# A two-layer relational graph convolution: six treatments of TensorE at its signals in layer 2

## Chip, cores and metric

The kernel runs on one core of a Trainium2 chip. Times are device microseconds (us) of one execution; below, PE is TensorE's matmuls, PEld its weight loads, DVE is VectorE, ACT is ScalarE, POOL is GpSimd and SP is SyncE.

## The reference

12500 nodes with 128 features, 200000 edges sorted by their destination, 8 relations. Two layers of a relational graph convolution, each with a residual, then one more residual and a layer norm:

```python
def _rgcn_conv(x, src, dst, et, basis, comp, root, bias):
    W = jnp.einsum('rb,bio->rio', comp, basis)
    xw = jnp.einsum('ni,rio->nro', x, W)
    msgs = xw[src, et]
    seg = dst * N_REL + et
    summed = jax.ops.segment_sum(msgs, seg, num_segments=N_NODES * N_REL)
    cnt = jax.ops.segment_sum(jnp.ones((msgs.shape[0],), x.dtype), seg, num_segments=N_NODES * N_REL)
    mean = summed / jnp.maximum(cnt, 1.0)[:, None]
    agg = mean.reshape(N_NODES, N_REL, HIDDEN).sum(axis=1)
    return agg + x @ root + bias
...
for l in range(N_LAYERS):
    h_new = _rgcn_conv(h, src, dst, edge_type, basis[l], comp[l], root[l], bias[l])
    h_new = jax.nn.relu(h_new)
    h = h_new + h
...
x = _layernorm(x + h, axis=-1)
```

(The last line is the reference's, with the convolutions' result called h.)

## The kernel before

The edges lie in 1563 tiles of 128, and eight tiles make an octet: 196 octets in each layer. The kernel works through the octets in order, layer 1 and then layer 2. For each octet POOL issues eight indirect DMAs (`gather`, L677), each of which fetches 128 rows of 128 floats into a ring of seven buffers `rows`; a buffer is asked for again five octets ahead of its use. In layer 1 the rows come from `x`, and the means of each destination and relation are multiplied by the relation's weights. Layer 1 also makes the table `y_d`, in which every node's row is already multiplied by each of the eight weights, so layer 2 gathers rows of `y_d` and only has to average and add them.

In layer 2 an octet q below 192 (`FULL`) goes through these steps:

- DVE makes the one-hot matrices `sT` and `pl` two octets ahead (`slot_hots`, L1090 and L1093).
- `slot_sums(q)` (L1428) is eight fp32 matmuls (L1441; each is recorded as two passes) of `rows` with `sT` into one part of the bank `po`. The last of them signals. It waits for the gathers of the octet, for DVE, and for ACT's copy of the octet before, since all octets use the same part of the bank.
- ACT copies the sums to `ys` (L627, by `copy`), and signals.
- `place_sums(q)` (L1449) adds `ys` to the accumulator `s` of the current block of nodes with a matmul by `pl` (L1466), and at a block's end also the root term (L1470). It stands on PE one octet late: PE's order is `slot_sums(q)`, `place_sums(q-1)`, then `slot_sums(q+1)`.
- At the end of a block DVE takes the accumulator (L1298, L1302, L1322), and every eight blocks four transposes at a time on PE (L1573) and the layer norm on DVE follow.

A buffer of `rows` comes free for the next gather when `slot_sums` of its octet has signalled, so POOL waits on PE's signals, ACT waits on them for the copy, and DVE for its matrices and for the accumulators. POOL's next gathers stand behind a waiting one on its queue.

The order on each engine is that in which the Python code calls `plan.add`. `Plan` works out, for each operation, which counts of which engines it must wait for, and `Plan.emit` (L395 to L408) writes the waits, the operation, and, where a count is waited for, `then_inc` on the engine's semaphore: a signal that the operation itself sends as it completes. `plan.mark("PE")` makes the last operation added a signalling one. An operation of PE never waits for PE.

Of the kernel before, what the change touches and what calls it, by code (L numbers as in the profile page):

```python
# [300 lines left out]
class Plan:  # L301
# [25 lines left out]
    def add(self, eng, emit, reads=(), writes=(), lane=None, n=1, after=()):  # L327


        raw, war = {}, {}  # L330
        writes = list(writes) + [c for c in reads if c[0] in self.banks]

        def need(d, op):
            proc, at = self.ops[op][0:2]
            d[proc] = max(d.get(proc, 0), at)

        me = len(self.ops)
        for c in (*reads, *after):
            if c in self.writer:
                need(raw, self.writer[c])  # L340
        for c in writes:
            if c in self.writer:
                need(raw, self.writer[c])
            for op in self.readers.get(c, ()):
                need(war, op)
        for c in reads:
            self.readers.setdefault(c, []).append(me)
        for c in writes:
            self.writer[c] = me
            self.readers[c] = []  # L350
        if lane is not None:
            k, i = self.lanes[lane]
            proc = (lane, i)
            self.lanes[lane][1] = (i + 1) % k
            if self.count[proc]:
                need(war, self.last[proc])
            step = 16 * n
        else:
            proc, step = eng, 1
            if eng == "PE":  # L360
                raw.pop(eng, None)
                war.pop(eng, None)
        known = self.known[eng]
        waits = {}
        for d, exact in ((raw, True), (war, False)):
            for p, at in d.items():
                if known.get(p, 0) >= at or waits.get(p, 0) >= at:
                    continue
                if p in self.signals and (self.lazy or not exact):
                    later = [a for a in self.signals[p] if a >= at]  # L370
                    at = min(later) if later else at
                waits[p] = max(at, waits.get(p, 0))
        for p in list(waits):
            for o in waits:
                if o != p and self.seen[o, waits[o]].get(p, 0) >= waits[p]:
                    del waits[p]
                    break
        for p, at in waits.items():
            if p in self.signals:
                self.signals[p].add(at)  # L380
            for o, a in self.seen[p, at].items():
                known[o] = max(known.get(o, 0), a)
            known[p] = max(known.get(p, 0), at)
        self.count[proc] += step
        at = self.count[proc]
        self.seen[proc, at] = dict(known)
        if lane is not None:
            self.last[proc] = me
        self.ops.append((proc, at, eng, emit, waits))

    seen = None
    last = None
    banks = ("ps", "py", "po", "pt", "ct")

    def emit(self):  # L395
        value = {e: {a: i + 1 for i, a in enumerate(sorted(s))} for e, s in self.signals.items()}
        end = max(i for i, op in enumerate(self.ops) if op[2] == "SP")
        for i, (proc, at, eng, emit, waits) in enumerate(self.ops):
            if i == end:
                self.landed(False)  # L400
            for p, a in sorted(waits.items(), key=str):
                self.engines[eng].wait_ge(self.sems[p], value[p][a] if p in value else a)
            ins = emit()
            if proc != eng:
                for x in ins if isinstance(ins, list) else [ins]:
                    x.then_inc(self.sems[proc], 16)
            elif at in value[eng]:
                ins.then_inc(self.sems[eng], 1)  # L408
    def landed(self, stores):

        for p in self.last:
# [18 lines left out]
def ordered_path(  # L430
# [25 lines left out]
    nc = tc.nc  # L456
# [31 lines left out]
    SOLO = 50  # L488
    FLAG = 100
    SOON = 16  # L490
    DONE = NT - 4
    FULL = NQ - 4
    assert D == P and R * K == P and B == BF + 1 and 1 < TL and LAST < P and BF % 4 == 0 and Q == G and N % 2 == 0
# [111 lines left out]
    nb_f = keep([1, 1], F32, "nb_f")  # L605

    plan = Plan(tc, {"hw": 8, "aq": 4, "gq": 4})
    plan.seen, plan.last = {}, {}

    def vec(emit, reads=(), writes=()):  # L610
        plan.add("DVE", emit, reads, writes)
# [4 lines left out]
    def pe(emit, reads=(), writes=()):  # L616
        plan.add("PE", emit, reads, writes)
# [815 lines left out]
    def slot_sums(q):  # L1433
        t, c = rows_g.pop((1, q))
        d, dc = dms2.pop(q)
        b, bc = misc
        m0 = b[:, 3, :]

        def emit():
            for i in range(Q):  # L1440
                last = nc.tensor.matmul(m0[i // 2 * 2 * K:(i // 2 + 1) * 2 * K, :], d[:, i, :], t[:, i, :],  # L1441
                                        start=i % 2 == 0, stop=i % 2 == 1)
            return last

        pe(emit, [c + (0,), c + (1,), dc], [bc, ("done", 1)])
        plan.mark("PE")
        o, oc = ys[q] = ys_r.take()
        copy(o, m0, [bc], [oc])
        plan.mark("ACT")  # L1449

    def place_sums(q, k, opens, last):
        t, c = pl.pop(q)
        o, oc = ys.pop(q)
        a, ac = acc[k]
        root_in = opens and k >= 0
        reads = [c, oc]
        m = P
        if root_in:
            ht, hc = hb[k]
            reads += [hc, ("w", 1, R)]  # L1460
        fixed = q == SOON // Q
        if fixed:
            reads += fix_rows_c + fix_dm_c

        def emit():
            ins = nc.tensor.matmul(a, o[:m], t[:m], start=opens, stop=last and not root_in and not fixed)  # L1466
            if fixed:
                ins = nc.tensor.matmul(a, fix_rows, fix_dm, start=False, stop=last and not root_in)
            if root_in:
                ins = nc.tensor.matmul(a[:, :rows_of(k)], w_sb[:, 1, R, :], ht[:, :rows_of(k)], start=False, stop=last)  # L1470
            return ins

        pe(emit, reads, [ac])
        plan.mark("PE")

    def add_rows(q, k, opens, last, between_last=None):
        t, c = rows_g.pop((1, q))
# [363 lines left out]
    for q in range(NQ):  # L1841
        near_end = q >= FULL
        if q == FLAG:
            load_flag()
        plan.lazy = not near_end
        k = sup(q)
        if gathers(1, q):
            pool(lambda: nc.gpsimd.drain())
        opens, last = opened_by(q)
        if opens:  # L1850
            acc[k] = acc_b[k % 2]
        if q == NQ - 1:
            last_st = st_r.take()
            turn, stats, one_by, scale = zip(*(last_norm(i) for i in range(2)))
            add_rows(q, k, opens, last, turn[0])
            stats[0]()
            for step in finish(1, k):
                step()
            turn[1]()
            one_by[0]()  # L1860
            stats[1]()
            scale[0]()
            one_by[1]()
            scale[1]()
            break
        if q == NQ - 2:
            first_sums()
        if q == 0:
            check_all()
        late = q - 1  # L1870
        if q < FULL:
            slot_sums(q)
        if 0 <= late < FULL:
            place_sums(late, sup(late), *opened_by(late))
        if q >= FULL:
            add_rows(q, k, opens, last)
        onehot(1, q + 2)
        if sup(q + 2) != sup(q + 1) and q + 2 < NQ:
            open_block(sup(q + 2))
        if todo:  # L1880
            todo.pop(0)()
        for i in range(2):
            for j, step in ending:
                step()
                plan.mark("DVE")
                n = j // S
                if j >= 0 and j % S == S - 1:
                    norm(n)
                    if n + 2 < NX:
                        todo.extend([lambda: None] * 2 + [lambda n=n: load_x(n + 2)])  # L1890
            ending.clear()
            if q == NQ - 2:
                if i == 0:
                    add, close_it, carry_on = finish(1, k, True)
                    for step in (carry_on, add, close_it):
                        step()
            elif i == 0:
                for j in [late] * (0 <= late < FULL) + [q] * (q >= FULL):
                    if opened_by(j)[1]:
                        a, b = finish(1, sup(j))  # L1900
                        a()
                        ending.append((sup(j), b))
            if not near_end:
                break
        while near_end and todo:
            todo.pop(0)()

# [64 lines left out]
```

## Time and profile before

| what | value |
|---|---|
| runs | 4581.87, 4591.37, 4590.76 us; median 4590.76 |
| the profiled execution | 4590.46 us, span 4588.4 us |
| granted TensorE clock, mean of the span | 0.665 |
| busy over the span | POOL 64%, PE 42%, PEld 33%, DVE 30%, ACT 10% |
| gathers of layer 2 | first at 2320.7, last at 4571.9 us |

The profile is of one execution. Its page gives each engine's busy time, the span in 40 slices (each digit a busy share in tenths; PEclk is the clock that the throttle granted to TensorE), and groups of instructions by line. A group's row has the busy time, the mean of one in ns, and the idle time of the engine just ahead of its instructions with what ended most of it; "remote" is a release that the profile puts down to none of the core's recorded instructions at that moment, and "issue" a wait for nothing that it shows. In the timeline a row is the start, the time taken, the engine, the line, the operation, and in brackets the idle time ahead of it. The end of a matmul is modelled.

### The profile page before, as it was taken

What the parts mean: (1) busy time and instruction counts of PE and PEld (TensorE: products, weight loads), DVE (VectorE), ACT (ScalarE), POOL (GpSimd) and SP (SyncE); (2) the same over time, 40 slices, a digit from 0 to 9 for tenths busy, and PEclk for the clock granted to TensorE, in tenths of its full rate; (3) what the DMA queues carried; (4) which work ended last, traced back from release to release, by engine and by line L of the source; (5) the groups of instructions that cost most, each with busy time, mean ns of one, the idle gap of its engine ahead of it and who ended that gap; (6) DMA issues with size and microseconds to landing.
All of it is one profiled execution on the core that took longest, in us unless ns stands there. A gap on an engine that the chain in (4) does not pass through costs nothing.

```text
span 4588.4 us, 33820 instructions
## 1 busy us (share of the span) xinstructions
PE 1941.5 (42%) x11751; PEld 1512.2 (33%) x11751; DVE 1384.9 (30%) x4891; ACT 466.3 (10%) x1141; POOL 2953.3 (64%) x3135
## 2 busy tenths in 40 slices
PE   2666756666566666656731122222222222222213
PEld 1555555555455555545521111111111111111112
DVE  2544333333333323233321222222222222222224
ACT  0111112121111111111210000000000000000000
POOL 5666666666666666666556666666666666666665
PEclk9878778787777777777865555555555555555556
DMA  3111122232222222222221111212212212122121
GB/s 100 45 50 46 46 62 87 87 92 92 88 69 73 74 69 74 64 66 70 78 71 45 47 51 52 56 46 57 55 47 55 56 47 56 46 56 55 47 55 50
DMA packets 129812, 284.69 MB, mean 62 GB/s; under 512 B 54019, under 2 KB 61773, under 8 KB 129637
## 3 DMA queue, kind: packets, MB, share of 16 engines
q0 software_dynamic: 100064, 205.13, 17.2%
q10 hardware_dynamic: 16971, 52.05, 3.0%
q1 hardware_dynamic: 12602, 25.31, 1.6%
q8 instruction: 94, 1.54, 0.1%
q14 instruction: 81, 0.66, 0.0%
HBM read 223.63 MB, written 58.65 MB: 62 GB/s over the span
## 4 chain that ended last, share of the span: by engine, by line
another core or an unknown queue 64%; PE 20%; issue 8%; ACT 5%; DVE 2%; DMA 0%; POOL 0%; SPq 0%; ACTq 0%; POOLq 0%; DVEq 0%
PE y L1246 7%; PE s L1214 5%; ACT sT L627 2%; PE pt L1345 2%; PE po L1441 2%; ACT ys L627 1%; PE po L1277 1%; DVE dm L1121 1%; ACT y_row L627 1%; PE ct L1345 1%; PE ct L870 0%; PE po L1279 0%; PE ct L871 0%; PE pt L1183 0%
## 5 line engine op out<-in xcount | busy, mean ns | idle before, releaser
L677 POOL DMA_INDIRECT rows<-in_x_dram,idx x1563 | 1476.1, 944 | 841.7 <-issue 440.2
L677 POOL DMA_INDIRECT rows<-y_d,idy x1563 | 1475.1, 944 | 742.6 <-issue 453.3
L1441 PE MATMUL po<-rows,sT 128*32 128x128 f32 x3072 | 206.3, 411 | 1571.3 <-ACT ys L627 1151.2
L1246 PE MATMUL y<-w_sb,sT 128*128 128x128 f32 x3136 | 542.3, 345 | 526.2 <-ACT ys L627 198.6
L1246 PEld LDWEIGHTS y<-w_sb,sT 128*128 128x128 f32 x3136 | 509.4, 254 | 551.6 <-ACT ys L627 207.6
L1121 DVE TENSOR_SCALAR dm<-cols,kr,w 128x128 f32<-128x128 f16 x1563 | 526.2, 403 | 494.2 <-remote 203.1
L1441 PEld LDWEIGHTS po<-rows,sT 128*32 128x32 f32 x3072 | 121.9, 155 | 1658.1 <-ACT ys L627 1190.5
L1090 DVE TENSOR_SCALAR sT<-cols,kr,w 128x32 f32<-128x32 f16 x1536 | 352.8, 303 | 762.9 <-remote 617.7
L1214 PEld LDWEIGHTS s<-dm,rows 128*128 128x128 f32 x3126 | 436.3, 217 | 161.0 <-ACT sT L627 86.5
L1214 PE MATMUL s<-dm,rows 128*128 128x128 f32 x3126 | 450.5, 302 | 64.9 <-ACT sT L627 40.8
L627 ACT ACTIVATE sT<-s 128x512 f32<-128x512 f32 x391 | 212.5, 596 | 783.0 <-remote 556.8
L627 ACT ACTIVATE ys<-po 128x128 f32<-128x128 f32 x192 | 53.2, 277 | 2087.1 <-remote 1936.5
L1298 DVE TENSOR_TENSOR s<-s,carry 128x128 f32<-128x128 f32 x97 | 28.9, 298 | 670.8 <-remote 455.7
L1298 DVE TENSOR_TENSOR po<-po,carry 128x128 f32<-128x128 f32 x98 | 29.2, 298 | 655.1 <-remote 454.7
L1345 PE MATMUL pt<-w_sb,arena 128*128 128x512 f32 x258 | 157.3, 682 | 62.4 <-issue 50.0
L1466 PE MATMUL s<-pl,ys 128*128 128x256 f32 x288 | 167.9, 684 | 0.0
L1277 PE MATMUL po<-pl,ys 128*128 128x256 f32 x392 | 139.4, 440 | 24.2 <-issue 15.8
L627 ACT ACTIVATE y_row<-pt 128x512 f32<-128x512 f32 x131 | 78.4, 598 | 682.0 <-remote 484.2
L870 PE MATMUL ct<-arena,id_h 128*128 128x512 f16 (+1 forms) x188 | 75.5, 421 | 84.4 <-DVE arena L860 37.1
L860 DVE TENSOR_TENSOR arena<-cols,arena 128x129 f16<-128x129 f16 (+62 forms) x188 | 73.6, 408 | 69.5 <-remote 65.5
L1129 DVE TENSOR_SCALAR pl<-cols,pos 128x256 f32<-128x256 f16 x196 | 93.1, 476 | 0.0
L1466 PEld LDWEIGHTS s<-pl,ys 128*128 128x128 f32 x288 | 69.7, 301 | 53.3 <-issue 53.3
(212 smaller groups left out, 1409.7 us busy)
## 6 DMA issues: line engine op xcount, KB each, us to landing
y_d<-y_row ACTq DMA_DIRECT2D x96, 512.0 KB
rows<-in_x_dram,idx POOLq DMA_INDIRECT x1563
rows<-y_d,idy POOLq DMA_INDIRECT x1563
x_g<-in_x_dram SPq DMA_DIRECT2D x24, 512.0 KB
out_dram<-x_g SPq DMA_DIRECT2D x12, 512.0 KB
arena<-in_L_gnn_basis_dram SPq DMA_DIRECT2D x2, 512.0 KB
w_d<-y_row SPq DMA_DIRECT2D x2, 512.0 KB
w_sb<-w_d SPq DMA_DIRECT2D x2, 512.0 KB
```

Source lines behind the costliest of these rows:

```text
L627: act(lambda: nc.scalar.activation(out_t, in_t, AF.Copy), reads, writes)
L677: ins.append(nc.gpsimd.indirect_dma_start(out=t[:, i - q * Q, :], out_offset=None, in_=table_t, in_offset=bass.IndirectOffsetOnAxis(ap=ids ...
L870: nc.tensor.matmul(ct[:, :nb, :], id_h, eq[:, s - s0, :nb, main], start=(s == 1), stop=False)
L1090: vec(in_turn([lambda i=i: nc.vector.tensor_scalar(t[:, i, :], cols[:, :2 * K], kr[:, i0 + i:i0 + i + 1], w[:, i0 + i:i0 + i + 1], op0=ALU ...
L1121: emits.append(lambda i=i: nc.vector.tensor_scalar(t[:, i - q * Q, :wide], cols[:, :wide], ids[:, i:i + 1], w[:, i:i + 1], op0=ALU.is_equa ...
L1129: emits.append(lambda: nc.vector.tensor_scalar(o[:m], cols[:m], pos[:m, g // (2 * R), g % (2 * R):g % (2 * R) + 1], None, op0=ALU.is_equal))
L1214: last = nc.tensor.matmul(s_b[i // 4][0][:, i % 4, :], t[:, i, :], d[:, i, :], start=True, stop=True)
L1246: last = nc.tensor.matmul(y[:m], t[:, r, :nt, :].rearrange("p t k -> p (t k)"), w_sb[:, 0, r, :], start=(r == 0), stop=(r == R - 1))
L1277: ins = nc.tensor.matmul(a, o[:m], t[:m], start=opens, stop=last and not root_in)
L1345: pe(lambda: nc.tensor.matmul(hb[:n].rearrange("p r d -> p (r d)"), hT[:, j * P:j * P + n], w_sb[:, 1, k * H:(k + 1) * H, :].rearrange("p ...
L1441: last = nc.tensor.matmul(m0[i // 2 * 2 * K:(i // 2 + 1) * 2 * K, :], d[:, i, :], t[:, i, :], start=i % 2 == 0, stop=i % 2 == 1)
L1466: ins = nc.tensor.matmul(a, o[:m], t[:m], start=opens, stop=last and not root_in and not fixed)
```

## The change

Layer 2's octets are put into six ranges by `kind(q) = min(q, 191) // 32`, 32 octets each. All other code stays, and so does the order of the instructions on every engine; PE gets additions or another way to signal:

| range | octets | what PE does |
|---|---|---|
| 0 | 0 to 31 | as before |
| 1 | 32 to 63 | after all other PE work of an octet's turn, 12 matmuls of `id_h` with itself (f16, 384 columns) into the bank `y`, which layer 2 doesn't use |
| 2 | 64 to 95 | at the same place, 36 weight loads of `id_h` |
| 3 | 96 to 127 | the signals of `slot_sums` and `place_sums` are sent by a `drain` that follows the matmuls, not by the last matmul |
| 4 | 128 to 159 | like range 1, with 4 matmuls |
| 5 | 160 to 191 | one weight load of `id_h` behind each `slot_sums` and each `place_sums` |

`place_sums` stands one octet late, so its range is that of the octet in whose turn it is. Over the whole, PE gets 512 matmuls, 1217 weight loads and 64 drains. None of the matmuls and weight loads signals or waits for another engine. The last four octets (192 to 195) are as before.

```diff
+        if eng == "PE" and self.settle:
+            self.settled.add(len(self.ops))
         self.ops.append((proc, at, eng, emit, waits))
...
             elif at in value[eng]:
-                ins.then_inc(self.sems[eng], 1)
+                if i in self.settled:
+                    self.engines[eng].drain().then_inc(self.sems[eng], 1)
+                else:
+                    ins.then_inc(self.sems[eng], 1)
...
+    BURST = 12
...
+        plan.settle = kind(q) == 3
         pe(emit, [c + (0,), c + (1,), dc], [bc, ("done", 1)])
         plan.mark("PE")
+        if kind(q) == 5:
+            load_on(1)
+        plan.settle = False
...
+        plan.settle = kind(q + 1) == 3
         pe(emit, reads, [ac])
         plan.mark("PE")
+        if kind(q + 1) == 5:
+            load_on(1)
+        plan.settle = False
...
+    def keep_on(n):
+        f = y_full[0]
+        rhs = id_h[:, None, :].to_broadcast([P, 3, P])
+
+        def emit():
+            for _ in range(n):
+                last = nc.tensor.matmul(f[:, :3, :], id_h, rhs, start=True, stop=True)
+            return last
+
+        pe(emit, ["id_h"], [y_full[1]])
+
+    def load_on(n):
+        def emit():
+            for _ in range(n):
+                last = nc.tensor.ldweights(id_h)
+            return last
+
+        pe(emit, ["id_h"], [])
+
+    def kind(q):
+        return min(q, FULL - 1) // 32
...
+        if q < FULL:
+            if kind(q) == 1:
+                keep_on(BURST)
+            if kind(q) == 2:
+                load_on(3 * BURST)
+            if kind(q) == 4:
+                keep_on(BURST // 3)
```

On PE, in range 1, two turns read as follows before (L1441 is the slot sums, L1466 and L1470 the place sums; a row's waits are those of its first matmul):

```order
L1441 MATMUL po_139<-rows_107,sT_112 32x128 [waits s_gq3,s_ACT]
L1441 MATMUL po_139<-rows_107,sT_112 32x128 x7
L1466 MATMUL s_135<-pl_115,ys_118 128x256 [waits s_DVE]
L1470 MATMUL s_135<-id_k,w_sb 128x128
L1441 MATMUL po_139<-rows_108,sT_112 32x128 [waits s_gq0,s_DVE,s_ACT]
L1441 MATMUL po_139<-rows_108,sT_112 32x128 x7
L1466 MATMUL s_135<-pl_116,ys_119 128x256
```

The same two turns of the changed kernel, whose lines for slot and place sums are L1449, L1478 and L1482, and whose L1498 is `keep_on`:

```order
L1449 MATMUL po_139<-rows_107,sT_112 32x128 [waits s_gq3,s_ACT]
L1449 MATMUL po_139<-rows_107,sT_112 32x128 x7
L1478 MATMUL s_135<-pl_115,ys_118 128x256 [waits s_DVE]
L1482 MATMUL s_135<-id_k,w_sb 128x128
L1498 MATMUL y<-id_h 128x384 x12
L1449 MATMUL po_139<-rows_108,sT_112 32x128 [waits s_gq0,s_DVE,s_ACT]
L1449 MATMUL po_139<-rows_108,sT_112 32x128 x7
L1478 MATMUL s_135<-pl_116,ys_119 128x256
L1498 MATMUL y<-id_h 128x384 x12
```

Nothing changed places; the twelve matmuls stand between a turn's place sums and the next turn's slot sums. In range 2 the row of L1498 is one of 36 weight loads. On PE in range 5 of the changed kernel (L1506 is `load_on`):

```order
L1449 MATMUL po_139<-rows_104,sT_112 32x128 x7
L1506 LDWEIGHTS id_h
L1478 MATMUL s_136<-pl_114,ys_117 128x256
L1506 LDWEIGHTS id_h
L1449 MATMUL po_139<-rows_105,sT_112 32x128 [waits s_gq3,s_DVE,s_ACT]
L1449 MATMUL po_139<-rows_105,sT_112 32x128 x7
L1506 LDWEIGHTS id_h
```

There a weight load stands directly behind each matmul that signals. In range 3 the rows read as before, with a drain behind each L1449 x7 and behind each turn's place sums.

More of the change, by code (lines that the diff above doesn't have):

```diff
@@ L392 @@
     last = None
+    settle = False
+    settled = None
     banks = ("ps", "py", "po", "pt", "ct")
@@ L607, in ordered_path @@
     plan = Plan(tc, {"hw": 8, "aq": 4, "gq": 4})
-    plan.seen, plan.last = {}, {}
+    plan.seen, plan.last, plan.settled = {}, {}, set()
     def vec(emit, reads=(), writes=()):
```

## The prediction

> **What bounds the kernel now.** I read the page's first two parts, to see which engine is full and where the stage of the change lies.
>
> ```profile
> span 4588.4 us, 33820 instructions
> ...
> PE 1941.5 (42%) x11751; PEld 1512.2 (33%) x11751; DVE 1384.9 (30%) x4891; ACT 466.3 (10%) x1141; POOL 2953.3 (64%) x3135
> ...
> PE   2666756666566666656731122222222222222213
> ...
> POOL 5666666666666666666556666666666666666665
> PEclk9878778787777777777865555555555555555556
> ```
>
> No engine is full. From slice 20 on, which is layer 2, TensorE is busy about two tenths at a granted clock of five tenths, and POOL, which issues the gathers, about six tenths. Two stretches of the stages, one of layer 1 and one of layer 2, give the work per octet, and POOL's group gives the price of a gather (eight to an octet):
>
> ```profile
> 400.00:1000.00 600.00, 381.50 (x2113) 321.02 (x2114) 217.35 (x663) 104.46 (x223) 390.42 (x414) 0.79 0.25 72
> 2500.00:4500.00 2000.00, 440.41 (x3432) 271.65 (x3432) 516.03 (x2141) 69.42 (x275) 1329.70 (x1410) 0.52 0.19 52
> ...
> L677 POOL DMA_INDIRECT rows<-y_d,idy x1410 | 1330.6, 944 | 670.5 <-issue 407.8 <-remote 261.1 <-PE po L1441 0.6
> ```
>
> The columns of the first two rows are the stretch and its length, then busy time and instructions of PE, PEld, DVE, ACT and POOL, then the clock. In layer 2 an octet takes 2000 x 8 / 1410 = 11.35 us. A gather is 0.944 us, and 407.8 us over 1331 waits, 0.306 us, lie between two: eight take 10.0 us. That is the floor of an octet; 1.35 us stand above it. What POOL waits for in these is in the list of waits of the same stretch (total, number, longest):
>
> ```profile
> ACT ys L627 <- remote: 1786.6, 123, 25.1
> ...
> PE po L1441 <- ACT ys L627: 1084.4, 73, 23.0
> ...
> POOL rows L677 <- issue: 407.8, 1331, 1.6
> POOL rows L677 <- remote: 261.1, 74, 5.8
> ```
>
> POOL is held up 74 times in 176 octets, once in 2.4 octets, for 3.53 us; less the 0.306 us that every issue has, 3.2 us, and 74 x 3.2 / 176 = 1.35 us an octet, which is the excess. The order of the instructions says for what: a ring buffer, free once the slot sums that read it have signalled. The timeline of one such place shows that the signal is late, not the work:
>
> ```profile
> 3298.74 0.90 PE L1441 MATMUL po<-rows,sT 128*32 128x128 f32 x12
> ...
> 3299.56 1.22 PE L1466 MATMUL s<-pl,ys 128*128 128x256 f32 x2
> ...
> 3310.09 0.94 POOL L677 DMA_INDIRECT rows<-y_d,idy  x1 [0.30 <-issue]
> ...
> 3316.52 0.28 ACT L627 ACTIVATE ys<-po 128x128 f32<-128x128 f32 x1 [17.85 <-remote]
> ...
> 3316.76 0.94 POOL L677 DMA_INDIRECT rows<-y_d,idy  x1 [5.72 <-remote]
> ...
> 3318.10 0.28 ACT L627 ACTIVATE ys<-po 128x128 f32<-128x128 f32 x1 [1.30 <-PE po L1441]
> ...
> 3319.04 1.10 PE L1441 MATMUL po<-rows,sT 128*32 128x128 f32 x16
> ...
> 3325.31 0.28 ACT L627 ACTIVATE ys<-po 128x128 f32<-128x128 f32 x1 [6.73 <-remote]
> ```
>
> The slot sums end at 3299.64, and their copy, the only thing that waits for their signal, begins at 3316.52, 16.9 us later. POOL issues gathers without a break until 3311.0, then stands still, and 5.5 us after that the copy, and then POOL, go on. The next octet's copy follows its sums closely; the one after, whose sums end at 3320.14 with POOL issuing again, 5.2 us late. Where gathers stand still for long (they wait for a table near the end) every signal is on time:
>
> ```profile
> 4511.13 1.10 PE L1441 MATMUL po<-rows,sT 128*32 128x128 f32 x16
> ...
> 4512.33 0.28 ACT L627 ACTIVATE ys<-po 128x128 f32<-128x128 f32 x1 [2.34 <-PE po L1441]
> ...
> 4512.84 0.67 PE L1441 MATMUL po<-rows,sT 128*32 128x128 f32 x16
> ...
> 4513.43 0.70 PE L1466 MATMUL s<-pl,ys 128*128 128x256 f32 x2
> 4513.60 0.28 ACT L627 ACTIVATE ys<-po 128x128 f32<-128x128 f32 x1 [0.80 <-PE po L1441]
> ...
> 4515.28 0.94 POOL L677 DMA_INDIRECT rows<-y_d,idy  x1 [10.62 <-PE po L1441]
> ```
>
> The two copies begin 0.10 and 0.09 us after the modelled end of their sums. So **the bound is a cycle**: POOL issues; TensorE's signals come late while it does; buffers run out, POOL stops; the signals arrive; a burst of some octets passes on TensorE, and POOL issues again. A range of 32 octets holds 32 x 1.35 = 43 us of stall, and that is all a range can win.
>
> **The change part by part.** Layer 1 asks whether PE work behind a signal brings it out, since it has more of it:
>
> ```profile
> 1495.28 1.95 PE L1214 MATMUL s<-dm,rows 128*128 128x128 f32 x16
> ...
> 1501.25 3.37 PE L1246 MATMUL y<-w_sb,sT 128*128 128x128 f32 x16 [4.03 <-issue]
> ...
> 1508.14 0.62 PE L1345 MATMUL pt<-w_sb,arena 128*128 128x512 f32 x1 [2.11 <-issue]
> ...
> 1511.03 0.60 ACT L627 ACTIVATE sT<-s 128x512 f32<-128x512 f32 x1 [9.84 <-remote]
> ...
> 1511.27 0.94 POOL L677 DMA_INDIRECT rows<-in_x_dram,idx  x1 [3.25 <-remote]
> ```
>
> The sums of L1214 end at 1497.23. Sixteen matmuls of 3.37 us and others run from 1501.25 on; the copy of the sums still begins only at 1511.03, again when POOL has stood still. Work behind the signal did not fetch it, and I take it that the unused work of this change doesn't either: in ranges 1, 2, 4 and 5 the 43 us stay. What is left is the price of the work.
>
> The price of layer 2's added instructions comes from the nearest rows in f16:
>
> ```profile
> L870 PE MATMUL ct<-arena,id_h 128*128 128x512 f16 (+1 forms) x188 | 75.5, 421 | 84.4 <-DVE arena L860 37.1
> ...
> L870 PEld LDWEIGHTS ct<-arena,id_h x188: 95/147/153, 12.1 to 555.2; 128*128 128x128 f16 x188
> ```
>
> The 188 are 141 of 512 columns and 47 of 128, so 78208 columns in 75.5 us, 0.97 ns each; a matmul of 384 columns is 0.37 us by estimate, twelve 4.5 us, four 1.5 us. 36 weight loads at the median of 147 ns are 5.3 us. None has a wait or a signal, so no other engine waits for them directly; the cover is TensorE's idle time. By the stretch of layer 2, 440.41 of 2000 us are busy, so an octet has 11.35 - 2.5 = 8.8 us idle, mostly in the wait for a late copy. **The cover is gone in the burst** after a stop, where one octet's copy follows its sums by under a microsecond and the next octet's sums would stand behind the unused work.
>
> How much that costs is bounded from both sides. Layer 1 is a stage with the same cycle and more PE work: 414 gathers in 600 us are 11.59 us an octet, with 381.50 / 51.75 = 7.37 us of busy PE, against 11.35 with 2.50. That is 0.24 us an octet for 4.87 us of work, 0.05 us per us. At the other end, unused work that shortens the burst from 2.4 octets to 1.4 per stop makes the stall 3.2 / 1.4 = 2.3 us an octet, 0.94 more, 30 us a range. Below nothing it goes only if signals come earlier, which are rivals. I take layer 1's end, since it is a measured stage: range 1, 4.5 x 0.05 x 32 = **+7 us**; range 2, 5.3 x 0.05 x 32 = **+8**; range 4, **+2**; range 5, two loads an octet, 0.3 us, **+0.5**.
>
> The clock has a rule that speaks for the unused work. In the Trainium skill, "TensorE: Matmul & The Clock Gate", section "Part 1: The HAM clock gate", some 3.4 us of sustained work bring the full clock and an idle window of that length takes it away. The trace agrees in kind: slot sums take 1.11 us in most of layer 2 and 0.67 at 4512.84, after two microseconds of dense work. What it would give is a rival below.
>
> Range 3, drains: each slot sum and each place sum is followed by an instruction that waits until TensorE is empty and then signals. No drain of TensorE is in the trace. If it signals at the time when the matmul would have, the slot sums' lateness now also holds the place sums that stand behind it: before, they ran at once (L1466 at 3299.56, right behind L1441); now they run after the release, inside the burst, 1.22 us and up to 0.64 of L1470 for an octet whose sums take 1.11. From below it costs nothing, where the lateness is passed elsewhere; from above it is a burst of 1.4 octets again, +30. I take a burst of 2.0 instead of 2.4, since an octet's 2.2 us in the burst grow by a part of a microsecond for two drains: 3.2 / 2.0 - 1.35 = 0.25 us an octet, 32 x 0.25 = +8, and 2 us for the drains themselves, **+10**.
>
> Sum, against the profiled execution: 4590.46 (span 4588.4) + 7 + 8 + 10 + 2 + 0.5 = **4618 us**. The median of the runs is 4590.76, so nothing needs to be shifted.
>
> **The rivals.**
> A, *drains signal on time* (ends faster). If the lateness belongs to how a matmul's completion is reported, and a drain that finds the array empty reports for itself, range 3 loses its 43 us and the others keep their price: 4590.5 - 43 + 17.5 = 4565. It decides the sign from the point where range 3 wins more than the 17.5 us of the others. For it: at 4512.33 a copy finds the results 0.10 us after the sums, and at 3316.52 and 3316.76 ACT and POOL go on within 0.24 us of one another, as if one late report had released both. Against: a drain must learn of the same completions.
> In the Trainium skill, "Perfetto Trace Analysis", section "Per-engine timelines", a matmul's update is pushed when PSUM has acknowledged the bytes, after an end that is only modelled, while a drain's is pushed by the sequencer. No row of this trace tells the two apart; by that page alone A or my forecast could hold.
> B, *unused work fetches the signals*: 43 us each in ranges 1, 2 and 4, with 10.5 left for 3 and 5: 4590.5 - 129 + 10.5 = 4472. Layer 1's row at 1511.03 is against it.
> E, *the clock*: full clock in ranges 1 and 2 makes slot sums 0.44 us and place sums 1.22 - 0.70 = 0.52 us shorter; were all of it on the path, 0.96 x 64 = 61 us, 4590.5 - 61 + 12.5 = 4542. Against: layer 1 has a clock of 0.79 against 0.52 and takes 11.59 us an octet.
> C, *added instructions are themselves delivered late*: at 1508.14 a matmul waited 2.11 us for nothing the profile shows. One such stall of 1.7 us for every twelve instructions, uncovered, is 54 us in range 1, 163 in range 2, 18 in range 4, 9 in range 5, 10 in 3: about 4845. Against: layer 1's slope.
> D, *it does nothing that matters*: all of it lies in the 8.8 us of idle time, drains included: 4590.
>
> **How the numbers follow.** A measurement of this kernel tells about 0.2%, 9 us, from no change. Chances: the forecast 0.48, A 0.17, D 0.17, C 0.09, B 0.06, E 0.03. Faster are A, B and E, 0.26; the same is D, 0.17; slower the forecast and C, 0.57. The forecast's own range is 4600 (layer 1's prices without the drains') to 4692, with every price at its upper end: +30 each for ranges 1, 2 and 3, +10 for range 4 in proportion, +2 for 5. The whole range goes from 4540 to 4700: it takes in A, D and E and leaves out B and C, 0.15.
>
> **What would show it.** With the time of each range of 32 octets taken by POOL's gathers in the trace after (about 362 us each before), the forecast wants 364 to 372 in ranges 1, 2 and 4, range 5 unchanged, about 372 in range 3, and POOL's waits on remote as long as now in all. A shows as some 320 us in range 3 with the copies of `ys` within a microsecond of the drains; B as 320 in 1, 2 and 4; E as a clock near 0.8 there and slot sums of 0.67 us with a shorter range; C as issue waits ahead of L1498 and L1506 and ranges 1 and 2 far over 400 us. The forecast is wrong, above all, if signals come on time in any range, and then by about 43 us.

## The result, and the profile after

The changed kernel takes 4595.22 us in the median of twelve runs, the kernel before 4590.87 on the same chip: a ratio of 1.0017, with a 95% interval of 1.0005 to 1.0029, so 2 to 13 us more where 27.5 were forecast. The profiled execution has a span of 4600.7 us, 12.3 more than that of before; 5.7 of these lie ahead of layer 2, where nothing was changed.

The page's first lines, after:

```profile
span 4600.7 us, 36125 instructions
...
PE 2071.9 (45%) x12263; PEld 1633.2 (35%) x13480; DVE 1384.8 (30%) x4891; ACT 466.1 (10%) x1141; POOL 2960.7 (64%) x3135
```

PE has 130 us more of busy time, and it is hardly to be seen in the span. POOL's group and the waits of the same stretch of layer 2 as before (2500 to 4500 us):

```profile
L685 POOL DMA_INDIRECT rows<-y_d,idy x1403 | 1327.1, 946 | 673.8 <-issue 403.7 <-remote 210.9 <-PEq L413 47.0
```

```profile
ACT ys L635 <- remote: 1391.7, 89, 26.5
...
ACT ys L635 <- PEq L413: 351.2, 32, 21.6
...
POOL rows L685 <- remote: 210.9, 67, 5.6
...
PEld L1506 <- issue: 143.0, 204, 1.8
...
POOL rows L685 <- PEq L413: 47.0, 12, 4.5
...
POOL rows L685 <- PE po L1449: 6.7, 3, 6.1
...
POOL rows L685 <- PE s L1482: 4.5, 1, 4.5
```

L413 is the drain. POOL's waits for anything but "issue", with 0.9 us of smaller ones, are 270.0 us together, against 262.6 before. The copies' waits, whatever ended them, are 1946 us against 1929 before. The gathers in 2000 us are 1403 against 1410. By the start of each range's first gather, ranges 0 to 5 took 392.9, 367.3, 367.1, 364.4, 364.0 and 365.8 us after, 392.1, 362.3 to 364.4 in ranges 1 to 3, 361.2 and 371.0 before. No range won or lost more than 5.2 us.

What the added matmuls do is in the timeline of range 1:

```profile
2897.57 0.95 POOL L685 DMA_INDIRECT rows<-y_d,idy  x1 [0.30 <-issue]
2898.24 0.48 PE L1498 MATMUL y<-id_h 128*128 128x384 f16 x1 [1.62 <-issue]
...
2900.35 0.48 PE L1498 MATMUL y<-id_h 128*128 128x384 f16 x1 [1.63 <-issue]
...
2903.35 0.28 ACT L635 ACTIVATE ys<-po 128x128 f32<-128x128 f32 x1 [13.25 <-remote]
...
2903.59 0.94 POOL L685 DMA_INDIRECT rows<-y_d,idy  x1 [3.82 <-remote]
...
2907.47 2.11 PE L1498 MATMUL y<-id_h 128*128 128x384 f16 x12
```

While POOL issues, not only the signal is late: the unused matmuls, which wait for nothing, start 0.7 to 2.1 us apart here. They lie in front of a copy that comes at 2903.35 all the same, when POOL has stood still. Shortly after the stop, with POOL issuing again, twelve of them take 2.11 us. For range 2, a row of 36 weight loads, also just after a stop:

```profile
3201.83 1.78 PEld L1506 LDWEIGHTS <-id_h 128*128 128x128 f16 x36
```

### The profile page after: what moved, and what is told of

The parts are those of the page before. It is cut to its first block, busy times and chain, and to the rows that moved or that the text cites. A ratio compares the mean times of both kernels' runs of the same rounds, so it can differ in the third digit from the quotient of the medians.

```text
span 4600.7 us, 36125 instructions
## 1 busy us (share of the span) xinstructions
PE 2071.9 (45%) x12263; PEld 1633.2 (35%) x13480; DVE 1384.8 (30%) x4891; ACT 466.1 (10%) x1141; POOL 2960.7 (64%) x3135
## 4 chain that ended last, share of the span: by engine, by line
another core or an unknown queue 52%; PE 25%; issue 14%; ACT 5%; DVE 3%; PEldq 1%; PEld 1%; DMA 0%; POOL 0%; SPq 0%; ACTq 0%; POOLq 0%; DVEq 0%
PE y L1254 7%; PE s L1222 6%; ACT sT L635 2%; PE po L1449 2%; PE pt L1353 2%; PE y L1498 1%; PE po L1285 1%; ACT ys L635 1%; PE s L1478 1%; DVE dm L1129 1%; ACT y_row L635 1%; PE ct L1353 1%; DVE sT L1098 1%; PEldq L413 1%
## 5 line engine op out<-in xcount | busy, mean ns | idle before, releaser
L1449 PE MATMUL po<-rows,sT 128*32 128x128 f32 x3072 | 210.7, 396 | 1117.9 <-ACT ys L635 741.6
L1449 PEld LDWEIGHTS po<-rows,sT 128*32 128x32 f32 x3072 | 122.3, 150 | 1013.1 <-ACT ys L635 620.2
L1478 PE MATMUL s<-pl,ys 128*128 128x256 f32 x288 | 163.6, 661 | 172.1 <-issue 171.5
L1498 PE MATMUL y<-id_h 128*128 128x384 f16 x512 | 143.1, 417 | 56.1 <-issue 55.1
L1478 PEld LDWEIGHTS s<-pl,ys 128*128 128x128 f32 x288 | 68.3, 289 | 216.9 <-issue 216.7
L1506 PEld LDWEIGHTS <-id_h 128*128 128x128 f16 x1217 | 75.4, 106 | 147.6 <-issue 146.1
```

The source lines that it names most:

```text
L1498: last = nc.tensor.matmul(f[:, :3, :], id_h, rhs, start=True, stop=True)
```

## Experiments

The first four put one suspect in all of layer 2. Theory W says that the work hides in the wait, P has the prediction's prices, R says that the gathers have a limit of their own. Where no ratio is given, the time is that of one execution, and the argument goes by its trace.

**all_mm12, all_ld36, all_drains.** The edit is one line:

```diff
-        return min(q, FULL - 1) // 32
+        return 1
```

(2 for the loads, 3 for the drains.)

> Range 1's treatment (12 unused matmuls) in all 192 octets; nothing else differs from the kernel before. Theory W (the work hides in the wait for a late signal; per range of 32 octets it costs what range 1 shows in the trace after, 367.3 against 364.4 us): 6 x 3 = +18 us, 4600 to 4620. Theory P (the prediction's price, 7 us a range): +42 us, about 4633. Rival R (layer 2's time is a limit of the gathers themselves, which PE doesn't touch): within 6 us of before.

> Range 2's treatment (36 weight loads) in all 192 octets. Theory W (367.1 against 362.3 us in the one range): 6 x 5 = +29 us, 4610 to 4630. Theory P (8 us a range): +48 us, about 4639. Rival R: within 6 us of before.

> Range 3's treatment (a drain sends the signals of slot sums and place sums) in all 192 octets. Theory W (a drain is as late as the matmul and costs nothing, 364.4 against 363.8 us in the one range): within 8 us of before, copies of ys as late as now (mean 7 to 10 us behind the slot sums). Theory P (10 us a range for the place sums that are held behind the drain): +60 us, about 4650. If drains were on time: -43 x 6 = -258 us, about 4330.

Measured against 4615.26 us of before on that chip: 4648.23 for the matmuls (ratio 1.0067, 1.0048 to 1.0086), 4659.43 for the loads (1.0084, 1.0061 to 1.0107), 4621.68 for the drains (1.0013, 0.9999 to 1.0027). That is 31 us for the matmuls (22 to 40), 39 for the loads (28 to 49) and 6 for the drains (-0.5 to 12.5). The matmuls lie between W and P, the loads between them or at P, the drains at W. R, which wanted all three within 6 us of before, misses the matmuls and the loads: the work on PE does cost something. POOL's group in the stretch from 2500 to 4500 us of all_mm12:

```profile
L685 POOL DMA_INDIRECT rows<-y_d,idy x1388 | 1310.1, 944 | 690.3 <-issue 394.2 <-remote 294.6 <-PE po L1611 0.9
```

the same of all_ld36:

```profile
L685 POOL DMA_INDIRECT rows<-y_d,idy x1383 | 1305.3, 944 | 695.4 <-issue 392.1 <-remote 303.2
```

and waits of all_drains in that stretch, with one stop in its timeline:

```profile
ACT ys L635 <- PEq L413: 1872.7, 169, 21.6
...
POOL rows L685 <- PEq L413: 267.7, 63, 4.7
```

```profile
3311.88 0.94 POOL L685 DMA_INDIRECT rows<-y_d,idy  x1 [0.30 <-issue]
3317.12 0.28 ACT L635 ACTIVATE ys<-po 128x128 f32<-128x128 f32 x1 [21.32 <-PEq L413]
...
3317.14 1.22 PE L1478 MATMUL s<-iota_f,ys 128*128 128x256 f32 x2 [19.14 <-issue]
3317.35 0.94 POOL L685 DMA_INDIRECT rows<-y_d,idy  x1 [4.52 <-PEq L413]
```

The drains are as late as the matmuls were (ACT waits 1873 us for them), and PE, POOL and ACT go on together. The place sums do stand behind the drain, as forecast, and POOL's stops are longer, 267.7 / 63 = 4.2 us against 3.5, but there are fewer of them, 63 against 74, so that they come to nearly the same sum.

The drains also show where the lateness sits. The profile records how long a drain stays on PE's sequencer (shortest, median and longest in ns):

```profile
L413 PEldq DRAIN  x384: 1007/2128/43127, 2395.6 to 4587.5; - x192
```

The one ahead of the copy at 3317.12 lasts from 3297.10 to 3317.08, and the longest ends 42 us after the modelled end of the last matmul ahead of it. In this trace a copy that waited follows the end of a drain by 0.04 us throughout. So the signal doesn't lose its time on the way to the other engines: TensorE itself isn't done until then. Whether its matmuls really end so late, or only their completion is told late inside it, stays open, since the end of a matmul is modelled.

**two_banks.** The slot sums alternate between two banks:

```diff
-        b, bc = misc
+        b, bc = (misc, y_full)[q % 2]
```

> The kernel before, with none of the six treatments; the slot sums of odd octets go to the bank y instead of po, so the slot sums of q+1 needn't wait for ACT's copy of q. Theory W (the pace of layer 2 is the chain slot sums, late signal, copy, next slot sums; a late report may serve two octets at once): POOL's stops shrink, and layer 2 goes from 11.35 us an octet toward the 10.0 us of POOL's issue: -100 to -240 us, 4350 to 4490. Rival R (a limit of the gathers themselves): 0, 4590.

Measured: 4616.23 us, ratio 0.9998 (0.9984 to 1.0011). The chain of slot sums, copy and next slot sums was loosened by one octet, and nothing came of it. It wasn't cut: PE now waits for the copy at the place sums, 842.0 us at L1466 in the same stretch, where before it waited 1084.4 at L1441. POOL's group:

```profile
L677 POOL DMA_INDIRECT rows<-y_d,idy x1404 | 1324.6, 943 | 676.5 <-issue 405.5 <-remote 251.7 <-PE y L1441 13.5
```

W, as the pace of layer 2, forecast 100 us or more to be won and falls, as far as one octet of room can tell; R forecast nothing, and nothing came. The next three take the two sides apart.

**free_gathers.** The slot sums read a fixed tile, so that no gather waits for PE, and PE for no gather:

```diff
+        mine = [c + (0,), c + (1,)]
+        if q > SOON // Q:
+            t = sT_r.tiles[1].rearrange("p r g k -> p (r g k)").rearrange("p (i d) -> p i d", i=Q)
+            mine = [("sT", 1, h) for h in range(2)]
...
-        pe(emit, [c + (0,), c + (1,), dc], [bc, ("done", 1)])
+        pe(emit, mine + [dc], [bc, ("done", 1)])
```

> The kernel before, but in layer 2 the slot sums of octets 3 to 191 read a fixed tile and not the gathered rows (so the sums are of other numbers), and nothing waits for TensorE to free a gather's buffer; every gather is still issued. Theory S (TensorE is held up while gathers are in flight, and POOL's stops are when it gets on): POOL issues without a stop at 10.0 us an octet, and TensorE falls behind, slower than 11.35 us an octet until the gathers end, then under 4 us an octet. Rival R (the gathers have a limit of their own of 11.35 us an octet): POOL still stops, about 1.35 us an octet, and TensorE's signals matter to nothing.

Measured: 4975.93 us, beside 4586.77 of before. POOL's group and two waits from 3000 to 4000 us, then a place in the timeline:

```profile
L677 POOL DMA_INDIRECT rows<-y_d,idy x716 | 769.7, 1075 | 232.0 <-issue 232.0
```

```profile
ACT ys L627 <- remote: 971.6, 18, 66.9
...
PE po L1445 <- issue: 837.9, 18, 53.7
```

```profile
3133.00 1.09 POOL L677 DMA_INDIRECT rows<-y_d,idy  x1 [0.30 <-issue]
3134.40 1.09 POOL L677 DMA_INDIRECT rows<-y_d,idy  x1 [0.30 <-issue]
3134.82 0.28 ACT L627 ACTIVATE ys<-po 128x128 f32<-128x128 f32 x1 [55.72 <-remote]
...
3135.15 1.11 PE L1445 MATMUL po<-sT,sT 128*32 128x128 f32 x16 [53.74 <-issue]
```

Both S and R were right in part. PE is starved: 18 octets in 1000 us, 55 us each, and once the gathers had ended 137 copies came in 400 us, 2.9 us each. But POOL, which waits for nothing at all here, doesn't run at 1.25 us a gather. It slows to 1000 / 716 = 1.397 us, 11.2 us an octet. **The octets of the kernel before, 11.35 us each, are not 1.35 us above a floor of 10.0, they are 0.15 us above one of 11.2.** It does not slow at once. From its last wait at 2368.71 us on it still issues one in 1.25 us, while PE's signals are already held: three copies come from 2400 to 2590 us. POOL's group in that stretch:

```profile
L677 POOL DMA_INDIRECT rows<-y_d,idy x153 | 144.7, 946 | 46.6 <-issue 46.6
```

The first gather that takes longer is at 2595.49, some 180 gathers after the wait. So POOL can run ahead of the price of 1.40 us for that many, and then must keep to it.

**half_gathers.** Four gathers of eight are left out:

```diff
+        elif l == 1 and SOON // Q < q < FULL:
+            plan.add("POOL", some(i0, i0 + 4), reads, [cell + (0,), cell + (1,)], lane="gq", n=4, after=after)
```

> The kernel before, with four of the eight gathers left out in octets 3 to 191 of layer 2 (half of the rows are stale). POOL's floor is 5.0 us an octet. Theory S: signals come in the quiet that POOL leaves; if the quiet per octet is a fixed 1.35 us, 6.4 us an octet; if TensorE's own chain (2.5 to 4 us) is the limit then, POOL stops longer but the octet stays under 7 us. Rival L (a signal's lateness is a fixed property of TensorE's signals, about 9 us an octet, whatever POOL does): about 10 to 11 us an octet. Rival R: half the gathers, half the time, 5.7 us.

Measured: 3529.67 us. From 2500 to 3300 us:

```profile
L677 POOL DMA_INDIRECT rows<-y_d,idy x554 | 524.2, 946 | 276.6 <-issue 149.4 <-remote 115.9 <-PE s L1468 5.9
```

800 / 554 = 1.444 us a gather, 5.8 us an octet: half the gathers, half the time, as R said. L falls: PE's signals come twice as often if half as much is gathered.

**hw_loads, hw_eight, pool_plain.** What in the gathers holds PE up? The same bytes come by one load from SP's queue, by eight from SP's, by eight plain DMAs from POOL's:

```diff
+        elif l == 1 and SOON // Q < q < FULL:
+            r0 = q * 500
+
+            def plain():
+                return [nc.gpsimd.dma_start(t[:, i, :], y_d[r0 + i * P:r0 + (i + 1) * P, :]) for i in range(Q)]
+
+            plan.add("POOL", plain, reads, [cell + (0,), cell + (1,)], lane="gq", n=Q, after=after)
```

> The kernel before, with the gathers of octets 3 to 191 of layer 2 replaced by one load each from SP's queue, of as many bytes in as many 512-byte rows from consecutive places of the table (other rows than asked for). Theory S with POOL's issue as the cause: TensorE's signals are on time (copies under 1.5 us behind the slot sums), and an octet takes 3 to 6 us, set by the loads. If any DMA traffic into the buffers delays them: copies several us late as now.

> The kernel before, with the eight gathers of octets 3 to 191 of layer 2 replaced by eight plain DMAs from POOL's queue, one tile each from consecutive rows of the table (other rows than asked for). Theory I (it is POOL's issue of the software queue that holds TensorE up): the copies are late as now or about so, several us. Theory X (only the indirect form does it): copies under 1.5 us behind the slot sums. An octet is then as long as eight issues take on POOL, which no trace has yet.

> As hw_loads, but eight loads of one tile each from SP's queue, so that as many transfers with as many completion signals as the gathers have run in each octet (other rows than asked for). Theory I (POOL's issue is the cause): copies under 1.5 us behind the slot sums, as in hw_loads, and an octet of 3 to 5 us, set by SP's issue. Theory N (the number of completion signals in the air is the cause): copies several us late.

Measured: 2992.24, 3253.45 and 3216.76 us. Two groups of pool_plain from 2500 to 3100 us:

```profile
L696 POOL DMA_DIRECT2D rows<-y_d x1143 | 601.0, 535 | 0.0
```

```profile
L627 ACT ACTIVATE ys<-po 128x128 f32<-128x128 f32 x143 | 39.7, 278 | 546.2 <-PE po L1448 546.2
```

and one octet in its timeline:

```profile
2701.62 1.10 PE L1448 MATMUL po<-rows,sT 128*32 128x128 f32 x16 [1.66 <-DMA rows<-y_d]
...
2702.80 0.28 ACT L627 ACTIVATE ys<-po 128x128 f32<-128x128 f32 x1 [4.08 <-PE po L1448]
```

POOL issues without pause, with as many transfers and completions, and the copy begins 0.08 us after the slot sums; "remote" is gone from ACT's waits. hw_loads and hw_eight show the same. An octet takes 600 / 143 = 4.2 us here. So neither the traffic into the buffers, nor the number of completions, nor POOL's queue as such is the cause. **The indirect form is** (theory X), or what comes with it: the gathers read scattered rows and the plain DMAs consecutive ones, and no run takes these two apart.

**deep_ring.** An eighth buffer, and gathers six octets ahead:

```diff
-        if o + AHEAD < NQ - LATE:
-            gather(l, o + AHEAD)
+        if o + AHEAD + l < NQ - LATE:
+            gather(l, o + AHEAD + l)
...
-    for q in range(AHEAD):
+    rows_r.tiles.append(sT_all[1].rearrange("p (i d) -> p i d", i=Q))
+    for q in range(AHEAD + 1):
```

> The kernel before with an eighth buffer for gathered rows in layer 2 (a tile that only layer 1 uses) and gathers issued six octets ahead. Theory G (a gather has a price of 1.40 us of its own, paid either at the issue or in the next stop; a stop costs about 0.6 us more): stops fewer by up to a third, 0.6 us each on 74, at most -15 us; within 0.3% of before. Theory S alone (stops are lost time, and a deeper ring would bridge them): -50 us or more.

Measured: 4613.39 us, ratio 0.9991 (0.9979 to 1.0003). G holds: the trace has 61 stops in the stretch from 2500 to 4500 us, and more room for them gives nothing that these rounds can tell from none.

**all_ld1, all_mm4.** The last two treatments everywhere (`return 5`, `return 4`):

> Range 5's treatment (one weight load behind each slot sum and each place sum) in all 192 octets. In the trace after, range 5 took 365.8 us against 371.0 us before; if that is the treatment's doing, 6 x -5 = -30 us, clearly faster than before. Theory W (the work hides, and the 5 us are what one trace differs from the next): within 8 us of before.

> Range 4's treatment (4 unused matmuls) in all 192 octets, the last term of the sum that was not measured. In proportion to all_mm12 (+31 us of 4615): +10 us. If four matmuls (1.5 us) vanish in the wait for a late signal: within 5 us of before. The prediction's price, 2 us a range: +12 us.

Measured: 4588.23 us beside 4586.77 (ratio 1.0000, 0.9986 to 1.0015) and 4623.81 beside 4619.54 (1.0011, 0.9999 to 1.0022). The 5.2 us that range 5 seemed to win were what one trace differs from the next.

**half_rows, half_rows_b.** Every gather fetches 64 rows of its 128:

```diff
+            def narrow():
+                return [nc.gpsimd.indirect_dma_start(
+                    out=t[:P // 2, i, :], out_offset=None, in_=table_t,
+                    in_offset=bass.IndirectOffsetOnAxis(ap=ids[:P // 2, i0 + i:i0 + i + 1], axis=0)) for i in range(Q)]
```

> The kernel before, with all eight gathers of octets 3 to 191 of layer 2 issued, but each for 64 of its 128 rows (the other half is stale). In free_gathers a gather of 128 rows settled at 1.40 us from issue to issue, in the kernel before 1.25 us plus a stop now and then, 1.42 us on average. If that price goes by the instruction: 1.40 us on average again, 11.3 us an octet, and copies as late as now. If it goes by the rows: well under 1.25 us, an octet of 6 to 9 us, and copies less late.

> half_rows again, since the chip of that run delays nothing: the kernel before took 3926.6 us there against 4590 here. On a chip where the kernel before takes about 4600 us: if a gather's price of 1.40 to 1.42 us goes by the instruction, 11.3 us an octet and copies as late as now; if by the rows, an octet of 9.6 us, which is what eight issues took in half_rows, and copies within a microsecond of the slot sums.

The first came to a chip that behaves otherwise (last section) and decides nothing on the price. The second, on a chip where before took 4619.54 us: 4627.19 us. From 2500 to 4500 us:

```profile
L694 POOL DMA_INDIRECT rows<-y_d,idy x1400 | 1259.7, 900 | 741.7 <-issue 406.6 <-remote 281.2 <-PE po L1448 42.5
```

A gather of half the rows is issued 0.05 us sooner, and POOL's stops are longer by as much: 2000 / 1400 = 1.429 us a gather again. The price goes by the instruction, as far as two sizes tell.

**What sets the pace.** A gather costs 1.40 us (free_gathers). POOL can issue it in 0.944 + 0.306 = 1.25, and then owes 0.15, which it pays in the next stop; each stop costs about 0.6 us on top. In 2000 us of layer 2 that gives, against the stops of the waits less 0.306 us each:

| kernel | gathers | stops | 0.15 x gathers + 0.6 x stops | measured stops, us |
|---|---|---|---|---|
| before | 1410 | 74 | 256 | 238 |
| all_drains | 1403 | 63 | 248 | 248 |
| all_mm12 | 1388 | 92 | 263 | 266 |
| all_ld36 | 1383 | 96 | 265 | 274 |
| half_rows_b, with 0.20 for 0.15 | 1400 | 67 | 320 | 315 |

The 0.6 was fitted to these rows, the 1.40 was measured apart from them. The table is a weak test: the measured stops are nearly what is left of 2000 us after the gathers at 1.25 us, before is 18 us off, and all_ld1, which isn't in it, would be 17 off. The stops one by one are a stronger one. Sorted by the gathers issued since the last stop (n), and less 0.306 us each, they take from 2500 us on:

| trace | n | stops | mean, us | 0.15 x n + 0.6 |
|---|---|---|---|---|
| half_gathers | 12 | 51 | 2.3 | 2.4 |
| all_drains | 16 | 5 | 3.0 | 3.0 |
| all_drains | 24 | 54 | 4.2 | 4.2 |
| before | 32 | 15 | 5.3 | 5.4 |

What is not paid in one stop comes in the next: before has stops of 1.33 us behind 24 gathers and 4.14 behind the 8 that follow, together as much as one behind 32. So a stop goes by the gathers ahead of it, and the added work on PE hardly moves it.

The debt is not in the transfers. In the trace of before the last packet of a gather ends 2.2 us after POOL's issue begins (median of the 1410; nine in ten under 2.3), at the end of a run of 32 as at its start. Why an indirect DMA has this price, and what it holds in PE, no run shows. The record has a granted clock for every execution, so all were recorded by the profiler as they ran; whether the recording has a part in it, no run shows either.

## Why the prediction was wrong, step by step

- **Right:** signals late while gathers are issued, and on time when none are. Right that unused work does not fetch them (A, B and E got nothing), that a drain is as late as the matmul, that range 5 does nothing, and that a higher clock wins nothing that can be seen: it was 0.64 from 2756 to 3123 us, in range 1, against 0.51 before from 2744 to 3108. "The signal is late, not the work" goes further than its rows: the drains are late themselves, inside TensorE.
- **Wrong, the step "That is the floor of an octet":** 10.0 us is POOL's issue while it is in debt, and not a rate that it can hold. The floor is 11.2 us (free_gathers). There were never 43 us to win in a range, only 0.15 us an octet, 0.15 x 32 = 5, so the rivals' times were out of reach by their size alone, whatever PE did.
- **Wrong, the step that failed the sum: range 3's "3.2 / 2.0 - 1.35 = 0.25 us an octet".** It took POOL's stop for a fixed 3.2 us, shared by the octets of a burst. The stop is a debt in proportion to the gathers since the last one, and the drains did not make stops more frequent either: all_drains has one in 1403 / 8 / 63 = 2.8 octets, not in 2.0. All drains together cost a ratio of 0.0013 (-0.0001 to 0.0027), 6 us, 1 us in a range, where 10 were forecast. That is 9 of the 14 us by which the sum was too high. The trace of before could have said so: stops of 2.8 us behind 16 gathers and 5.4 behind 32 are both in it, and only their mean was used.
- **Somewhat too large, and right in part by luck: ranges 1 and 2.** By the rounds of all_mm12 and all_ld36 a range costs 31 / 6 = 5.2 us with the matmuls (3.7 to 6.6) and 39 / 6 = 6.5 with the loads (4.7 to 8.2), for 7 and 8 forecast; in the trace after it is 2.9 and 4.8. Two errors offset each other: 12 matmuls were priced at 4.5 us and take 2.11 just after a stop, 36 loads at 5.3 and take 1.78, but a microsecond of such work costs more than layer 1's 0.05 us, by these numbers 5.2 / (2.11 x 32) = 0.08 and 6.5 / (1.78 x 32) = 0.11. POOL stops more often in these traces (92 and 96 times; 77 in two_banks on the same chip), which at 0.6 us a stop gives 9 and 11 us in 2000, where the stops grew by 19 and 26; the rest has no shown cause.
- **Range 4:** a ratio of 0.0011, 5 us over six ranges, 0.8 for 2.
- The sum of the measured terms, 5.2 + 6.5 + 1 + 0.8 + 0 = 13.5 us, lies at the upper end of the change's own interval of 2 to 13, and within the noise of both.
- **Rival C's mechanism was there** (unused matmuls 2.1 us apart at 2898.24), and nearly free: they waited beside a signal that was just as late. What was priced as uncovered, 54 us in range 1, was covered but for 5.
- **D, no effect that matters,** came nearest, with 0.17 of the chance, though 2 to 13 us are not nothing. Its reason, idle time of PE, holds for most of the unused work. What it leaves out is that layer 2 goes at the gathers' own pace, which is why the drains cost so little.
- **Two slips that change nothing:** layer 1's prices without the drains' give 4590.5 + 17.5 = 4608 as the lower end of the forecast's own range, not 4600; and the dense work ahead of the quick slot sums at 4512.84 begins at 4508.52, so it is 4.3 us long and not two.

## What to carry to other kernels

Before a stall is counted as time to be won, let the stalled engine run with nothing to wait for: here POOL then slowed by itself to nearly the pace it had with its stops. Let it run long enough, too: for its first 180 gathers it looked as if the stops were all there was to win. A wait that moves with the work since the last one, and not with what it waits for, was here a debt of the waiting engine. And where a signal is late, ask what runs on other engines in that moment before changing the engine that sends it.

## What the runs showed of the hardware

- While POOL issues indirect DMAs back to back, TensorE's instructions and signals hardly get on, but for a few microseconds after a stop: an octet of 2.9 us took 55 us (free_gathers). The time passes inside TensorE, where a drain lasted up to 43 us (all_drains). ScalarE's signals are not held so: its copy ends at 3135.10 there, and PE starts at 3135.15. Plain DMAs of the same bytes from the same queue hold nothing (pool_plain: 0.08 us). The Trainium skill, "DMA: Bandwidth & Descriptors", section "SWDGE vs HWDGE vs iDMA", tells that POOL's direct and indirect DMAs alike are made by software on GpSimd, which writes their descriptors into rings; pool_plain and the gathers thus share that path, and only one of them delays TensorE, so what the section describes doesn't by itself explain it.
- An indirect DMA has a price of 1.40 us by the instruction, for 128 rows as for 64; a plain DMA of 128 rows from POOL took 0.525 us (1143 in 600 us).
- This is not so on every chip. On the one that ran half_rows the kernel before took 3926.6 us, and half_rows 3861.99, where the same kernel took 4627.19 as half_rows_b. In half_rows' trace, layer 1, which has its full gathers, from 400 to 1000 us, and layer 2 from 2500 to 3300:

```profile
L677 POOL DMA_INDIRECT rows<-in_x_dram,idx x481 | 454.7, 945 | 146.6 <-issue 145.4 <-PE ct L1352 0.6 <-PE po L1286 0.3
```

```profile
L694 POOL DMA_INDIRECT rows<-y_d,idy x664 | 597.6, 900 | 202.6 <-issue 202.6
```

The same stretch of layer 1 in the kernel before, on the chip of the first profile:

```profile
L677 POOL DMA_INDIRECT rows<-in_x_dram,idx x414 | 390.9, 944 | 212.3 <-issue 114.6 <-remote 70.5 <-PE s L1214 27.2
```

There POOL holds 600 / 481 = 1.247 us a gather with no stop, here 1.449 with stops, and in layer 2 the copies aren't late (the one at 2708.49 begins 0.06 us after its slot sums). Both layers pay the price. By estimate from these paces it is (0.20 + 0.17) x 1563 = 580 of the 664 us between the two chips' times of the kernel before (0.17 is 1.42 less 1.25 in layer 2). The change itself was not run there, and what differs between the chips no run shows.
